# Neighbour search in segments, all aligned aggregation tiles on VectorE, longer lists in two blocks, one-hots on ScalarE

## The chip, the cores and the metric

The kernel runs on one core of one Trainium2 chip. The metric is the device time of one execution in microseconds (us); the median of several executions counts. One execution was also recorded by the hardware profiler. TensorE (PE in the profile) multiplies matrices, VectorE (DVE), ScalarE (ACT) and GpSimd (POOL) work elementwise, SyncE (SP) issues DMA transfers; GpSimd also issues the indirect DMA transfers (gathers).

## The reference

```python
# layer 0: graph convolution; adj is 2048 x 2048, sparse, random weights, diagonal present
A_norm = A + eye(n)
deg = A_norm.sum(0) + A_norm.sum(1) - diagonal(A_norm)
A_hat = A_norm * deg[:, None]**-0.5 * deg[None, :]**-0.5
agg = einsum('nm,bmd->bnd', A_hat, x)                  # x: 8 x 2048 x 256
h = relu(batchnorm(agg @ W1.T + b1)); o = batchnorm(h @ W2.T + b2)
x = layernorm(x + o)
# layer 1: attention over the neighbours only, 4 heads of 64
q, k, v = split(x @ W)
scores = q @ k.T / 8 + where(adj == 0, -inf, 0)
x = layernorm(x + softmax(scores) @ v)
```

All is fp32. Rows with small numbers have many neighbours, later rows few, since the edge probability falls with both indices.

## The kernel before

The 2048 nodes are cut into 16 blocks of 128 rows. Blocks 0 and 1 (`DENSE = 2`) are aggregated by a dense product; blocks 2 to 15 through lists of neighbours. In layer 1, block 0 attends densely and blocks 1 to 15 through the lists.

A list has two kinds of entries, called tiles; one tile is one gather of 128 rows. `ELL[t]` tiles of block t are *aligned*: tile i holds the i-th neighbour of each of the 128 rows. What rows have beyond `ELL[t]` neighbours is packed into `CAP[t]` *left-over* tiles, in which each partition belongs to some row of the block; for those a 128x128 one-hot matrix, made from the row numbers `qi1`, puts each entry back into its row. `LISTS` holds (ELL, CAP) for each block.

The order of instructions on each engine is the order in which the program writes them (`manual_schedule`); small generators are advanced by `next(...)` at chosen places. The stages, with their place in the profiled execution:

- **First stage, 0 to 72 us.** Sixteen 1 MB pieces of the adjacency matrix are loaded (L412) into 16 slots of 8 KB per partition. ScalarE and TensorE add up rows and columns (L416, L435). From the fourth piece on, one search step is taken for each piece (L442). Then a VectorE copy of the column sums (L447) starts the short sequence that gives `dinv` (L458, the inverse roots of the degrees), and the lists of blocks 2 and 3 are made (`list_steps`).
- **Dense product, 72 to 184 us.** For each of 16 pieces of x: load, scale by `dinv` (L472), store to `xs_d` (L473), 16 matrix instructions (L476). Two or three search steps go with each piece (L480).
- **Aggregation through lists and first linear layer, 184 to about 600 us** (pool `l0`). A loop over 116 tiles. Each tile gathers 128 rows of 8 KB from `xs_d` (L537) into a free slot. A tile that is *mine* is accumulated by VectorE in one pass over 128x2048 elements (L608 for the first of a block, L612 for the others); any other goes through TensorE with a weighted one-hot or diagonal matrix (L621, 8 instructions). `on_vector(t)` says how many aligned tiles of a block VectorE takes. At a block's end `add_rows` (L355) joins both parts, and `turn_steps` and `linear_steps` (transposes L394, products L377, statistics L371) are queued; `do_work(1 + mine)` advances them at each tile. One search step is taken at each tile (L588) as long as any is left. `gather_ahead` issues up to 10 gathers ahead, while enough slots are free; a block's slot is free once its search is done.
- **Second linear layer, about 600 to 830 us** (pool `l1`), with the seven-product scheme: `W[1]` to `W[4]` are sums and differences of quarters of W2, made on GpSimd (L667 to L670) from `w2s`, which is loaded at the stage's start (L656).
- **Attention, 830 to 2202 us.** Four passes of two batch entries each, and in a pass one step for each of 132 tiles. `score` (L1213 product, L1215 reduction, on VectorE) works 5 tiles ahead, `exps` (L1224, ScalarE) 4 ahead, `weigh_values` 3 ahead: the left-over tile's one-hot (L1230, VectorE) and the weighted values, on ScalarE for two of five tiles (three of five in the last pass; eight instructions, L1239) and else on VectorE (one instruction, L1244). `add_up` (L1255, TensorE) adds the tile to its rows. Keys and values are gathered 10 tiles ahead (L1195), queries of left-over tiles too (L1201). Projections of the next pass and the attention of block 0 are spread over the steps as side tasks.

**The search before.** `search_steps` handles one block after the other, 2 to 15 and then 1. It overwrites the block's rows by descending numbers where an edge is (L219), then takes `ROUNDS[t]` rounds over all 2048 columns: the eight largest (`max`, L223), and between rounds their removal (`match_replace`, L226). Each of these is one step: 2 x `ROUNDS[t]` steps for a block, 80 in all.

Of the kernel before, what the change touches and what calls it, by code (L numbers as in the profile page):

```python
# [27 lines left out]

LISTS = (
    None,  # L30
    (9, 7), (9, 5), (8, 3), (8, 2), (6, 3), (7, 2), (6, 2), (6, 2),
    (4, 3), (5, 2), (5, 2), (5, 2), (6, 1), (4, 2), (4, 2),
)
MAXNB = 32
ROUNDS = (0, 4, 3, 3, 3, 3, 3, 3, 3, 3, 2, 2, 2, 2, 2, 2)


@with_exitstack
def tile_gcn_then_masked_attention(
# [69 lines left out]
    idx = cpool.tile([P, NCOL], I32, name="idx")  # L109
    idxq = cpool.tile([P, NEDGE], I32, name="idxq")  # L110
    qi1 = cpool.tile([P, NEDGE], F32, name="qi1")
    padb = cpool.tile([P, NCOL], F32, name="padb")
    lbad = cpool.tile([P, 1], F32, name="lbad")
    iota_q1 = cpool.tile([P, P], F32, name="iota_q1")
# [64 lines left out]
    small = left.enter_context(tc.tile_pool(name="small", bufs=1, side="left", reuse_waits="tile"))  # L179
    st1 = small.tile([P, NH, NALL, 6], F32, name="st1")  # L180
    w1s = small.tile([P, ND, H], F32, name="w1s")
    over = small.tile([P, 3, NT], F32, name="over")
    lists = middle.enter_context(
        tc.tile_pool(name="lists", bufs=1, side="left", reuse_waits="tile")
    )
# [28 lines left out]
    def search_steps():  # L214

        for t in (*range(2, NT), 1):
            s = rows_of.pop(t)
            a = s.t
            nc.vector.scalar_tensor_tensor(a, a, 0.0, down, op0=ALU.not_equal, op1=ALU.mult)  # L219
            yield  # L220
            for r in range(ROUNDS[t]):
                m8 = nbx[:, t, 8 * r : 8 * r + 8]
                nc.vector.max(out=m8, in_=a)  # L223
                if r + 1 < ROUNDS[t]:
                    yield
                    nc.vector.match_replace(out=a, in_to_replace=m8, in_values=a, imm_value=0.0)  # L226
                else:
                    s.done()
                yield

    def list_steps(t, psum, name):

        r, m, cap, e0 = ELL[t], 8 * ROUNDS[t], CAP[t], edge0[t]
        here = slice(t, t + 1)
        ell = slice(col0[t], col0[t] + r)
        left_over = slice(col0[t] + r, col0[t] + r + cap)
        cols = slice(col0[t], col0[t] + r + cap)
        edges = slice(e0, e0 + cap)
# [26 lines left out]
        nc.vector.scalar_tensor_tensor(  # L265
            oh, iota_e[:, : cap * P], end[:, here], oh, op0=ALU.is_lt, op1=ALU.mult
        )
        yield
        yield
        pg = psum.tile([P, cap, MAXNB + 2 - r], F32, name=name)  # L270
        for i in range(cap):
            nc.tensor.matmul(
                pg[:, i, :], oh[:, i * P : (i + 1) * P], nbx[:, t, r:], start=True, stop=True
            )
        yield
        rank = lists.tile([P, cap], F32, name="rank")
        nc.vector.tensor_sub(rank, epos[:, :cap], pg[:, :, MAXNB - r])
        nc.vector.tensor_copy(qi1[:, edges], pg[:, :, MAXNB + 1 - r])
        for i in range(cap):
            c = left_over.start + i  # L280
            nc.vector.scalar_tensor_tensor(
                junk()[:, : m - r], iota_r[:, : m - r], rank[:, i : i + 1], pg[:, i, : m - r],
                op0=ALU.is_equal, op1=ALU.mult, accum_out=val[:, c : c + 1],
            )
        nc.vector.tensor_scalar(
            padb[:, cols], val[:, cols], 0.0, MASKED, op0=ALU.is_equal, op1=ALU.mult
        )
        key = lists.tile([P, MAXNB], F32, name="key")[:, : r + cap]
# [12 lines left out]
        nc.vector.scalar_tensor_tensor(  # L301
            fidx[:, left_over], q, float(N), key[:, r:], op0=ALU.mult, op1=ALU.add
        )
        nc.vector.tensor_scalar(wgt[:, ell], key[:, :r], rowid[:, here], None, op0=ALU.is_equal)
        nc.vector.tensor_tensor(wgt[:, left_over], key[:, r:], q, op=ALU.is_equal)
# [8 lines left out]
        )  # L314

    def on_vector(t):
        return 3 if t < 4 else ELL[t]

    def weights(t):

# [78 lines left out]
    with tc.tile_pool(name="first", bufs=1, side="right") as fp, tc.manual_schedule(  # L399
# [5 lines left out]
        with tc.tile_pool(name="pst", bufs=4, space=PSUM) as pst, tc.tile_pool(  # L405
# [3 lines left out]
            for t in range(NT):  # L409
# [29 lines left out]
                if not t:  # L439
                    rows_of.pop(0).done()  # L440
                if t > 2:
                    next(search)  # L442
            nc.sync.dma_start(w1s, w1t.rearrange("(c p) f -> p c f", p=P))
            for dst, src in params:
                nc.sync.dma_start(dst, src)
# [18 lines left out]
        with tc.tile_pool(name="ps_b", bufs=1, space=PSUM) as ps_b:  # L464
            pa = [banks(p) for p in (ps_a, ps_b)]
            for m in range(NT):
# [7 lines left out]
                for t in range(DENSE):  # L474
                    for c in range(QC):
# [1 line left out]
                            pa[t][c], at[:, t, m, :], xt[:, c * CH : (c + 1) * CH],  # L477
                            start=(m == 0), stop=(m == NT - 1),
                        )
                for _ in range(2 + m % 2):  # L480
                    next(search)
                if m < ELL[2] + CAP[2]:
                    gather_value(col0[2] + m)
                if m < ELL[3] + CAP[3]:
# [2 lines left out]
                weights(t)  # L487
            for t in range(DENSE):
                scale_rows(t, pa[t])

    with tc.tile_pool(name="l0", bufs=1, side="right", reuse_waits="tile") as lp, tc.tile_pool(
        name="psh", bufs=4, space=PSUM
# [78 lines left out]
        def turn_steps(t):  # L571
            for g in range(B // 2):
                turn_rows(t, g, psh)
                yield

        owed[0] = DENSE
        for _ in turn_steps(0):
            pass
# [6 lines left out]
        VLEAD, making = 16, []  # L585
        for n in range(len(tiles)):
            t, r, col, e, mine, k, count = tiles[n]
            next(search, None)  # L588
            for u in range(4, NT):
                if n == max(0, first[u] - VLEAD - 12):  # L590
                    making.append(list_steps(u, psh, "ph"))
# [42 lines left out]
            else:  # L634
                do_work(1 + mine)
        assert not making
        for f in work:
            for _ in f:
                pass
# [5 lines left out]
    with tc.tile_pool(name="l1", bufs=1, side="right", reuse_waits="tile") as lp, tc.tile_pool(  # L645
# [4 lines left out]
            for r in range(2):  # L650
                nc.sync.dma_start(hin[n][r].t, h_d[pairs[n][r]].rearrange("p f n -> p (f n)"))

        w2s = [lp.tile([P, 2, O], F32, name=f"w2s{j}") for j in range(2)]
        w2f = [lp.tile([P, 2, P], F32, name=f"w2f{j}") for j in range(4)]
        for j in range(2):
            nc.sync.dma_start(  # L656
                w2s[j], w2t[j * 2 * P : (j + 1) * 2 * P].rearrange("(c p) f -> p c f", p=P)
            )
        for n in range(TPC, TPC + 3):
            read_h(n)  # L660

        def w_half(i, j):
            return w2s[j][:, :, i * P : (i + 1) * P]

        W = {ij: w_half(*ij) for ij in HALVES}
        W[1], W[2], W[3], W[4] = w2f
        nc.gpsimd.tensor_add(W[1], W[1, 0], W[1, 1])  # L667
        nc.gpsimd.tensor_sub(W[2], W[1], W[0, 0])
        nc.gpsimd.tensor_sub(W[3], W[0, 0], W[1, 0])
        nc.gpsimd.tensor_sub(W[4], W[0, 1], W[2])  # L670

        st2 = lp.tile([P, NO, NALL, 6], F32, name="st2")
        bn1 = BatchNorm(lp, st1, g1s, be1s, sc1, sh1, "1")
# [118 lines left out]
            bn2.affine(o)  # L792
        nc.vector.tensor_reduce(lbad, over.rearrange("p a b -> p (a b)"), AX.X, ALU.add)

    left.close()


# [61 lines left out]
    def attention():  # L859

        with ExitStack() as st:
# [364 lines left out]
            def weigh_values(n):  # L1226
                e = tiles[n % NG][3]
                if e >= 0:
                    oh[n] = ep.tile([P, P], F32, name="oh", bufs=6)
                    nc.vector.tensor_scalar(  # L1230
                        oh[n], iota_q1, qi1[:, e : e + 1], None, op0=ALU.is_equal
                    )
                wv[n] = ep.tile([P, G2, NHEADS * VW], F32, name="wv", bufs=6)
                k, w = kg.pop(n), pw.pop(n)
                if n % 5 in (LAST_ON_ACT if n >= (NP - 1) * NG else ON_ACT):
# [467 lines left out]
```

## Time and profile before

| | |
|---|---|
| median of 14 runs | 2202.21 us (2199.77 to 2205.89) |
| the profiled execution | 2203.54 us, its span 2201.8 us |
| mean granted TensorE clock | 0.954 |
| busy share of the span | PE 90%, DVE 83%, POOL 66%, ACT 59% |
| DMA | 690.30 MB, mean 314 GB/s |
| search: L219, L223, L226 on VectorE | 34.1, 91.6 and 57.0 us busy |
| one-hots in attention, L1230 on VectorE | 160 instructions, 47.7 us busy |
| weighted values on ScalarE, L1239 | 1896 instructions, 477.3 us busy |

A matrix instruction of 128x512 elements shows about 0.6 us duration in the groups, but such instructions overlap: the chain of work that ended last shows eight of them (one tile, L621) in 3.43 us. In the same way a small VectorE or ScalarE instruction's duration is longer than the distance to the next one. So the distance between starts is read from the order of time where costs are added up.

### The profile page before, as it was taken

Reading aid. Unit: us, or ns where it says so; the run is one execution under the profiler, and the core shown is the slowest. Engines: PE = TensorE matmul, PEld = TensorE weight load, DVE = VectorE, ACT = ScalarE, POOL = GpSimd, SP = SyncE. Lnnn points to the kernel's source line nnn. Section 1 sums busy time; section 2 is a strip of 40 time slices with the busy share of each in tenths; the row PEclk is TensorE's granted clock in tenths of the full one; section 3 lists DMA queues with packets and bytes.
Section 4 is the critical chain, followed back from the end, with each engine's and each line's share of the span. In section 5 each row is a group of like instructions: output and inputs, shape, how many; then the busy total and the mean of one; then the engine's idle time right before and its main releaser. Section 6 shows DMA issues by size and latency. Waiting matters only on the chain.

```text
span 2201.8 us, 27916 instructions
## 1 busy us (share of the span) xinstructions
PE 1973.7 (90%) x7720; PEld 1277.9 (58%) x7720; DVE 1821.4 (83%) x3461; ACT 1302.0 (59%) x3896; POOL 1444.5 (66%) x1443
## 2 busy tenths in 40 slices
PE   5899989999999997979999999999999999687884
PEld 1444444445434444647776777777777777566663
DVE  6895999889856663229999999999999999989996
ACT  6331222223355534647777777877786877588875
POOL 2502668887457761137777787778786878878874
PEclk7899999999999998989999999999999999889996
DMA  8888899999648535569898999999999999999994
GB/s 323 287 306 308 342 344 354 356 382 405 249 174 288 168 87 205 193 244 338 329 371 331 355 354 365 363 339 379 325 365 349 358 355 340 349 372 359 332 346 152
DMA packets 261687, 690.30 MB, mean 314 GB/s; under 512 B 26385, under 2 KB 125457, under 8 KB 236433
## 3 DMA queue, kind: packets, MB, share of 16 engines
q0 software_dynamic: 109248, 442.68, 53.8%
q1 hardware_dynamic: 149968, 228.96, 29.3%
q10 hardware_dynamic: 2304, 16.78, 1.8%
q8 instruction: 64, 1.05, 0.2%
q14 instruction: 103, 0.84, 0.1%
HBM read 561.71 MB, written 126.62 MB: 313 GB/s over the span
## 4 chain that ended last, share of the span: by engine, by line
PE 48%; DVE 25%; ACT 8%; DMA 8%; issue 7%; POOL 3%; SPq 0%; DVEq 0%; ACTq 0%; POOLq 0%
PE pa L702 8%; PE ph L377 8%; PE pm L980 8%; DVE pr L1213 7%; PE pa L621 6%; PE po L1255 5%; PE pa L476 5%; ACT wv L1239 4%; DVE wv L1244 4%; DVE s L1215 4%; DMA kg<-kv_d,idx 2%; DMA e<-in_adj_dram 2%; DMA qg<-q_d,idxq 2%; ACT x L852 2%; POOL kg L1195 2%
## 5 line engine op out<-in xcount | busy, mean ns | idle before, releaser
L1195 POOL DMA_INDIRECT kg<-kv_d,idx x528 | 568.3, 1076 | 150.6 <-issue 81.3
L1239 ACT ACTIVATE wv<-kg,pw 128x65 f32<-128x65 f32 x1896 | 477.3, 336 | 0.0
L1255 PE MATMUL po<-wv,ident 128*128 128x260 f32 x1472 | 420.2, 399 | 49.1 <-DVE z L1069 47.6
L1215 DVE TENSOR_REDUCE s<-pr 128x8 f32<-128x512 f32 x528 | 362.1, 686 | 34.4
L980 PE MATMUL pm<-wq,x1t 128*128 128x512 f32 (+1 forms) x1024 | 374.4, 496 | 12.6 <-ACT x1t L925 12.4
L1255 PEld LDWEIGHTS po<-wv,ident 128*128 128x128 f32 x1472 | 276.9, 198 | 119.6 <-issue 69.8
L1224 ACT ACTIVATE pw<-s,padb 128x8 f32<-128x8 f32 x528 | 157.3, 299 | 223.2 <-DVE s L1215 221.9
L1213 DVE TENSOR_TENSOR pr<-qb,kg 128x512 f32<-128x512 f32 x368 | 260.1, 707 | 4.6 <-DMA kg<-kv_d,idx 2.5
L537 POOL DMA_INDIRECT e<-xs_d,idx x116 | 154.8, 1335 | 158.5 <-issue 82.9
L980 PEld LDWEIGHTS pm<-wq,x1t 128*128 128x128 f32 x1024 | 186.3, 192 | 104.2 <-issue 73.1
L377 PE MATMUL ph<-e,w1s 128*128 128x512 f32 x512 | 228.0, 593 | 0.8 <-ACT e L382 0.8
L1244 DVE TENSOR_TENSOR wv<-kg,pw 128x520 f32<-128x520 f32 x291 | 211.9, 728 | 2.4 <-ACT pw L1224 2.4
L1255 PE MATMUL po<-wv,oh 128*128 128x260 f32 x640 | 196.3, 397 | 8.7 <-DVE wv L1244 8.2
L1201 POOL DMA_INDIRECT qg<-q_d,idxq x160 | 164.5, 1028 | 48.8 <-issue 46.3
L311 POOL DMA_INDIRECT av<-in_adj_dram,fidx x116 | 154.4, 1331 | 44.1 <-issue 32.3
L382 ACT ACTIVATE h<-ph,b1s 128x512 f32<-128x512 f32 x96 | 66.0, 687 | 195.7 <-PE ph L377 194.6
L621 PE MATMUL pa<-e,wt 128*128 128x512 f32 x352 | 164.8, 612 | 0.0
L377 PEld LDWEIGHTS ph<-e,w1s 128*128 128x128 f32 x512 | 95.9, 190 | 115.4 <-issue 112.4
L1048 PEld LDWEIGHTS po<-kvr,p 128*128 128x128 f32 x1024 | 138.0, 198 | 30.9 <-ACT p L1037 21.8
L1029 PE MATMUL pm<-q,kt 128*128 128x256 f32 x512 | 137.6, 393 | 13.7 <-POOL q L932 9.4
L1048 PE MATMUL po<-kvr,p 128*128 128x65 f32 x1024 | 134.8, 276 | 15.4 <-ACT p L1037 15.2
L1255 PEld LDWEIGHTS po<-wv,oh 128*128 128x128 f32 x640 | 119.8, 198 | 38.0 <-issue 12.7
(190 smaller groups left out, 3362.5 us busy)
## 6 DMA issues: line engine op xcount, KB each, us to landing
kv_d<-kvr SPq DMA_DIRECT2D x32, 1032.0 KB, 6.9
h_d<-h SPq DMA_DIRECT2D x24, 1024.0 KB, 8.8
e<-h_d SPq DMA_DIRECT2D x24, 1024.0 KB, 7.2
e<-in_adj_dram SPq DMA_DIRECT2D x16, 1024.0 KB, 18.2
xt<-in_x_dram SPq DMA_DIRECT2D x16, 1024.0 KB, 7.9
xs_d<-xt ACTq DMA_DIRECT2D x16, 1024.0 KB, 7.4
y_d<-y SPq DMA_DIRECT2D x128, 128.0 KB, 2.2
yt<-y_d SPq DMA_DIRECT2D x32, 512.0 KB, 12.4
```

Of the source, the lines that this page charges most:

```text
L377: nc.tensor.matmul(ph, w1s[:, d, f * P : (f + 1) * P], as_agb(agb[t])[:, d, r * B // 2 : (r + 1) * B // 2, :], start=(d == 0), stop=(d == ...
L621: nc.tensor.matmul(pa[c], w, xg[n].t[:, c * CH : (c + 1) * CH], start=(k == 0), stop=(k == count - 1),)
L702: nc.tensor.matmul(py, w[:, f, :], t[:, f, :], start=(f == 0), stop=(f == 1))
L980: nc.tensor.matmul(pm, x1t[b, c][:, d, i * P : (i + 1) * P], rhs(d), start=(d == 0), stop=(d == ND - 1),)
L1048: nc.tensor.matmul(po0[b][:, h, :], p[:, h, :], heads(kvr[b, c][:, i, D:])[:, h, :], start=(j == 0 and h == 0), stop=(j == NT - 1), skip_g ...
L1195: nc.gpsimd.indirect_dma_start(out=kg[n].rearrange("p b e -> p (b e)"), out_offset=None, in_=kv_d[p][:], in_offset=bass.IndirectOffsetOnAx ...
L1201: nc.gpsimd.indirect_dma_start(out=qg[n].rearrange("p b e -> p (b e)"), out_offset=None, in_=q_d[p][:], in_offset=bass.IndirectOffsetOnAxi ...
L1213: nc.vector.tensor_mul(pr, q, kg[n][:, :, :D])
L1215: nc.vector.tensor_reduce(s.rearrange("p b h -> p (b h)"), pr.rearrange("p b (h e) -> p (b h) e", e=HD), AX.X, ALU.add,)
L1239: nc.scalar.activation(wv[n][:, b, hs], k[:, b, D:][:, hs], AF.Copy, scale=w[:, b, h : h + 1],)
L1244: nc.vector.tensor_mul(wv[n].rearrange("p b (h e) -> p b h e", e=VW), k[:, :, D:].rearrange("p b (h e) -> p b h e", e=VW), w[:, :, :, None ...
L1255: nc.tensor.matmul(po[p, t, b].rearrange("p h e -> p (h e)"), oh[n] if e >= 0 else ident, wv[n][:, b, :], start=(r == 0), stop=(r == ELL[t ...
```

## The change

- `search_steps` cuts the 2048 columns into 16 segments (12 for blocks from 10 on) and takes the eight largest of each by short `max` instructions into `best` (128x128 or 128x96); a reduction keeps the largest of the eighth values in `over[:, 3]`, so that a full segment is noticed at the end; the rounds then run over `best`. A block is four steps, 60 in all.
- Two search steps for each piece from the fourth on in the first stage (one before), three for each piece of the dense product (two or three before), none in the aggregation loop.
- `on_vector(t)` is `ELL[t]` for all blocks; it was 3 for blocks 2 and 3.
- `LISTS`: block 1 from (9, 7) to (12, 4), block 2 from (9, 5) to (10, 3). A pass has 131 tiles in place of 132, and 35 left-over tiles in place of 40.
- The one-hots of attention: two ScalarE instructions each, Square of (iota - qi1) and Relu of (1 - that), with the new `qn1 = -qi1`.
- `w2s` is loaded at the start of pool `l0`, and `W[1]` to `W[4]` are made at its end.

```diff
-    (9, 7), (9, 5), (8, 3), (8, 2), (6, 3), (7, 2), (6, 2), (6, 2),
+    (12, 4), (10, 3), (8, 3), (8, 2), (6, 3), (7, 2), (6, 2), (6, 2),
...
+SEGMENTS = (
+    (0, 8, 32, 72, 128, 200, 288, 392, 512, 648, 800, 968, 1152, 1352, 1568, 1800, 2048),
+    (0, 14, 57, 128, 228, 356, 512, 697, 910, 1152, 1422, 1721, 2048),
+)
...
+            parts = SEGMENTS[t >= 10]
+            n = len(parts) - 1
+            best = lists.tile([P, 16, 8], F32, name="best", bufs=2)[:, :n]
+            for i, (u, v) in enumerate(zip(parts, parts[1:])):
+                nc.vector.max(out=best[:, i, :], in_=a[:, u:v])
+                if i == n // 2:
+                    yield
+            s.done()
+            yield
+            nc.vector.tensor_reduce(over[:, 3, t : t + 1], best[:, :, 7], AX.X, ALU.max)
+            best = best.rearrange("p a b -> p (a b)")
             for r in range(ROUNDS[t]):
                 m8 = nbx[:, t, 8 * r : 8 * r + 8]
-                nc.vector.max(out=m8, in_=a)
+                nc.vector.max(out=m8, in_=best)
                 if r + 1 < ROUNDS[t]:
-                    yield
-                    nc.vector.match_replace(out=a, in_to_replace=m8, in_values=a, imm_value=0.0)
-                else:
-                    s.done()
-                yield
+                    nc.vector.match_replace(
+                        out=best, in_to_replace=m8, in_values=best, imm_value=0.0
+                    )
+            yield
...
+        nc.vector.tensor_scalar(qn1[:, edges], qi1[:, edges], -1.0, None, op0=ALU.mult)
...
     def on_vector(t):
-        return 3 if t < 4 else ELL[t]
+        return ELL[t]
...
                 if t > 2:
-                    next(search)
+                    for _ in range(2):
+                        next(search)
...
-                for _ in range(2 + m % 2):
-                    next(search)
+                for _ in range(3):
+                    next(search, None)
...
-            next(search, None)
...
-                    nc.vector.tensor_scalar(
-                        oh[n], iota_q1, qi1[:, e : e + 1], None, op0=ALU.is_equal
+                    nc.scalar.activation(
+                        oh[n], iota_q1, AF.Square, bias=qn1[:, e : e + 1]
                     )
+                    nc.scalar.activation(oh[n], oh[n], AF.Relu, bias=ones[:, :1], scale=-1.0)
```

More of the change, by code (lines that the diff above doesn't have):

```diff
@@ L111, in tile_gcn_then_masked_attention @@
     qi1 = cpool.tile([P, NEDGE], F32, name="qi1")
+    qn1 = cpool.tile([P, NEDGE], F32, name="qn1")
     padb = cpool.tile([P, NCOL], F32, name="padb")
@@ L181, in tile_gcn_then_masked_attention @@
     w1s = small.tile([P, ND, H], F32, name="w1s")
-    over = small.tile([P, 3, NT], F32, name="over")
+    over = small.tile([P, 4, NT], F32, name="over")
     lists = middle.enter_context(
@@ L489, in tile_gcn_then_masked_attention, with w_half @@
                 scale_rows(t, pa[t])
+    keep = ExitStack()
+    wp = keep.enter_context(tc.tile_pool(name="w2", bufs=1, side="right", reuse_waits="tile"))
+    w2s = [wp.tile([P, 2, O], F32, name=f"w2s{j}") for j in range(2)]
+    w2f = [wp.tile([P, 2, P], F32, name=f"w2f{j}") for j in range(4)]
+    def w_half(i, j):
+        return w2s[j][:, :, i * P : (i + 1) * P]
+    W = {ij: w_half(*ij) for ij in HALVES}
+    W[1], W[2], W[3], W[4] = w2f
     with tc.tile_pool(name="l0", bufs=1, side="right", reuse_waits="tile") as lp, tc.tile_pool(
@@ L574, in turn_steps @@
                 yield
+        for j in range(2):
+            nc.sync.dma_start(
+                w2s[j], w2t[j * 2 * P : (j + 1) * 2 * P].rearrange("(c p) f -> p c f", p=P)
+            )
         owed[0] = DENSE
@@ L636, in tile_gcn_then_masked_attention @@
         assert not making
+        nc.gpsimd.tensor_add(W[1], W[1, 0], W[1, 1])
+        nc.gpsimd.tensor_sub(W[2], W[1], W[0, 0])
+        nc.gpsimd.tensor_sub(W[3], W[0, 0], W[1, 0])
+        nc.gpsimd.tensor_sub(W[4], W[0, 1], W[2])
         for f in work:
@@ L651, in read_h @@
                 nc.sync.dma_start(hin[n][r].t, h_d[pairs[n][r]].rearrange("p f n -> p (f n)"))
[L653 to L658, printed above, removed]
         for n in range(TPC, TPC + 3):
             read_h(n)
[L662 to L670, printed above, removed]
         st2 = lp.tile([P, NO, NALL, 6], F32, name="st2")
@@ L793, in tile_gcn_then_masked_attention @@
         nc.vector.tensor_reduce(lbad, over.rearrange("p a b -> p (a b)"), AX.X, ALU.add)
+    keep.close()
     left.close()
```

## The prediction

> **What bounds the kernel now.** I read the chain of waits over the whole span, then the windows, then the order of time at the seams that the edits touch. A difference within 0.2% (4.4 us) can't be told from no change here.
>
> First stage, order of time on VectorE and what follows. Columns: start, duration, engine, line, and in brackets the idle time ahead with its releaser.
>
> ```profile
> 51.95 2.29 DVE L223 MAX8 nbx<-e 128x8 f32<-128x2048 f32 x1
> 54.16 2.27 DVE L219 SCALAR_TENSOR_TENSOR e<-e,down 128x2048 f32<-128x2048 f32 x1
> 57.21 0.69 DVE L447 COPY junk<-pc 128x512 f32<-128x512 f32 x1 [0.78 <-ACT junk L416]
> ...
> 62.39 2.00 ACT L472 ACTIVATE xt<-xt,dinv 128x2048 f32<-128x2048 f32 x1 [4.92 <-POOL dinv L141]
> ```
>
> The search ends at 56.43, just as the last adjacency piece has been summed; L447 is next in VectorE's order, and `dinv`, the lists and the dense product hang on it. There is no more than 0.8 us of slack: more search ahead of L447 moves everything behind.
>
> The dense product (72 to 184) is 256 matrix instructions in 111.7 us with PE busy all the time; work beside it is free. Then the aggregation, groups in the window 184 to 296, in which blocks 2 and 3 are aggregated (their last `add_rows` end at 248.4 and 298.3). Columns: line, engine, operation, count | busy us, mean ns | idle.
>
> ```profile
> L223 DVE MAX8 nbx<-e 128x8 f32<-128x2048 f32 x13 | 29.6, 2279 | 0.0
> L226 DVE MATCH_REPLACE8 e<-nbx,e 128x2048 f32<-128x2048 f32 x7 | 16.0, 2290 | 0.0
> L219 DVE SCALAR_TENSOR_TENSOR e<-e,down 128x2048 f32<-128x2048 f32 x5 | 11.4, 2277 | 0.0
> L612 DVE SCALAR_TENSOR_TENSOR e<-e,wgt,e 128x2048 f32<-128x2048 f32 x4 | 9.4, 2344 | 0.0
> L621 PE MATMUL pa<-e,wt 128*128 128x512 f32 x151 | 68.3, 595 | 0.0
> L377 PE MATMUL ph<-e,w1s 128*128 128x512 f32 x92 | 42.0, 593 | 0.0
> ```
>
> PE does mostly list tiles there, VectorE mostly search; from 184 to 260 the chain of waits is 98% PE (L621 59%, L377 32%, L394 7%). From block 5 on there is no search left and DMA runs at 0.95 to 1.0 with 380 to 420 GB/s: 28 us for 9 tiles. That part the change leaves alone.
>
> Attention: windows for passes 1 to 3 and the last pass (length, busy us of PE, PEld, DVE, ACT, POOL, granted clock, DMA share, GB/s), and the end of one tile's work in order of time.
>
> ```profile
> 1000.00:1870.00 870.00, 824.91 (x3964) 638.36 (x3963) 824.56 (x1699) 663.04 (x2289) 666.71 (x756) 0.99 0.95 352
> 1870.00:2180.00 310.00, 239.25 (x1078) 188.95 (x1076) 281.07 (x557) 242.60 (x925) 247.82 (x246) 0.89 0.94 337
> ```
> ```profile
> 1319.49 0.28 DVE L1230 TENSOR_SCALAR oh<-iota_q,qi 128x128 f32<-128x128 f32 x1
> ...
> 1319.69 0.69 DVE L1244 TENSOR_TENSOR wv<-kg,pw 128x520 f32<-128x520 f32 x1
> ```
>
> VectorE is busy 95% in the first three passes and has hardly any long wait (13 us of named waits in 870), so it sets the pace, with PE (95%) and DMA (0.95) close behind. ScalarE has a quarter free. A one-hot holds VectorE 0.20 us, from its start to the next one's.
>
> **Part by part.** *First stage, search.* What a short MAX8 costs no row shows. L265 takes 0.88 us at 640 columns and 0.48 at 256: 1.04 ns a column, so 2.13 us for 2048. A MAX8 of 2048 lasts 2.29, but the next independent instruction starts after 2.20 (184.83 to 187.03). So the fixed part of each segment is 0.07 (by distance) to 0.16 us (by duration); below that I allow zero. I take 0.07, since segments don't depend on each other. A step that needs the one before costs 0.19 extra (L256 to L257 to L258, one column each). A block of three rounds: 2.32 (L219) + 2.13 + 16 x 0.07 + 0.2 (reduction) + three maxima and two replacements of 128 columns at 0.32 and two value loads at 0.08 = 7.5 us, against 6 x 2.3 = 13.9 now; with two rounds 6.4 against 9.3. The 26 steps of the first stage are now blocks 2 to 7 whole and half of block 8: 6 x 7.5 + 3.6 = 48.6 us. They begin at 26.23 as now (after the copies L424) and end at 74.9, 18 us after today's 56.4; the adjacency has long landed, nothing hides it. Block 2's shorter left-over list (3 tiles, not 5) takes 1.6 us off the sequence from L447 to L476 (L262 0.54 to 0.41, L265 0.88 to 0.62, L272 ten instructions in 2.30 to six, two L281 at 0.15). **+16 us**; +5 if segments have next to no fixed cost, +26 with 0.16.
> The Trainium skill speaks against this edit: its page "VectorE: DVE Perf Modes", in the section on the TRN2 errata, says that small tiles pay a fixed latency each, 151 cycles by its measured formula, 157 ns. By that the 105 segments would cost 9 us more and the sum would end at 2177.
>
> *Dense product.* 34 steps are left, under 60 us of VectorE beside 112 us of PE; before, 40 steps were 92. Nothing on the path. If that cover were gone, it would be 60 us; it has 50 to spare.
>
> *Aggregation.* 27 full-width steps (62 us of VectorE) leave this loop, 12 aligned tiles go to VectorE (12 x 2.34 = 28 us), and 13 tiles (one is dropped) leave TensorE at 3.43 us each by the chain of waits: 45 us. Block 2, 64 us now: PE 3 x 3.43 + 16 products at 1.72 + transposes 2 + lists 1.6 = 41; VectorE 1.3 + 9 x 2.3 + 2.7 (L355) + 16 statistics at 0.61 + two lists at 3.7 + 1.4 = 43; DMA 13 tiles and 4 MB of `h` at 390 GB/s = 46, with a start of up to ten gathers instead of seven, as all search slots are free. These interlock: 48 us, saving 16 (10 to 20). Block 3, 50 us now: PE 28, VectorE 32, DMA 35: saving 15 (9 to 18). Block 4, 35 now: two search steps go, DMA wants 32: saving 3 (0 to 5). **-32 us** (-19 to -43 with the early gathers). What is late next is DMA.
>
> *Attention.* Per pass 5 left-over tiles and one tile less. VectorE: 160 one-hots x 0.20 = 32 us, 4 tiles at 1.8 (L1213, L1215, L1244) = 7: 39 in all, 29 of it in three passes where VectorE decides, 10 in the last. DMA: 20 x 262 KB + 4 x 528 KB = 7.3 MB, 20 us at 355 GB/s. ScalarE gains 140 pairs. The nearest rows for 128x128: 0.40 (L556), 0.29 (L417), and 0.25 between starts of 128x65 (eight in 2.01, L1239). The Relu needs the Square, so 0.5 to 0.8 a pair; I take 0.7: 98 us, 74 of it in 870, so ScalarE 76% to 88%; the last pass 78% to 86%, 92% in its middle (84% now). A pair stands in ScalarE's queue ahead of the next `exps` (L1224), on which VectorE's L1244 waits two steps later. Bounds: -36 if VectorE's time comes back whole, +12 if ScalarE's queue costs a third of a pair's time more than VectorE gives. I take **-18**: half of the 29, as PE and DMA stand at 0.95 too, and 3 in the last pass.
>
> *At no cost:* `qn1`, 15 instructions of 0.17 us under the list work; the `w2s` loads, on SP's queue now ahead of the first `h` store at 201 (their space is free at 184); W1 to W4 on POOL, 2.9 us, after the last gather as before (POOL idles 26 us ahead of L667), first used at 624.7.
>
> Sum against the profiled execution, 2203.5 (span 2201.8 and 1.7 around it): +16 - 32 - 18 = 2169.5; the median lies 1.3 below that execution: **2168**.
>
> **Rivals.** *More comes back:* VectorE's 36 in attention, segments cheap (+8), 40 in the aggregation: 2134 to 2145. For it: 13 us of waits in 870. Against: DMA at 0.95.
> *It cancels:* segments at 0.16 (+26), DMA holds blocks 2 and 3 (-19), attention -6: about 2203. For it: no short MAX8 is in the trace.
> *Slower: ScalarE's queue decides in attention.* From the point where the pair delays `exps` so that VectorE waits; ScalarE's reserve is its wait for L1215, 222 us in all. If half of the pairs' 98 us comes onto the path and half of the gain goes: +49 - 9 + 16 - 32 = +24, 2226. From a net loss of 16 in attention on, the kernel is slower. For it: in-order ScalarE at 92% in the last pass, with 2.0 us bursts (L1239). Against: 3 to 5 tiles of lead.
> *Table switches:* one row shows the price.
>
> ```profile
> L416 ACT ACT_TABLE_LOAD x1 | 1.3, 1283 | 0.8 <-PEq L1686 0.8
> ```
>
> One load serves Copy, Identity, Relu and Exp; Square is not in this trace. If it needed another table, 280 loads are 359 us of ScalarE, beyond its reserve: 2400 and more.
> The Trainium skill ("ScalarE: Activation LUTs", "Table sets: the hidden batching unit") names relu, copy, identity and abs as in every set, not square; by its 2.66 us a switch it would be 745 us.
>
> **How the numbers follow.** Forecast 0.56 (own range 2146 to 2192), more 0.17, cancels 0.10 (0.03 faster, 0.06 same, 0.01 slower), ScalarE 0.14, tables 0.03. Faster 0.76, same 0.06, slower 0.18. The range 2140 to 2208 leaves out the low half of "more" and most of the slower cases.
>
> **What would show it.** L447 near 75 instead of 57, the dense product 16 us later and as long; MAX8 of segments a mean distance near 0.2 us; the last `add_rows` of blocks 2 and 3 48 and 83 us after the dense product ends (64 and 114 now); no wait of VectorE for `exps`; one table load. Wrong if L447 stays, if block 2 keeps 60 us, or if VectorE waits for L1224.

## The result and the profile after

The changed kernel takes **2171.09 us** (median of 6 runs, 2166.06 to 2174.16); the kernel before, in 28 runs beside and ahead of it, takes 2203.22 us. The ratio is 0.9855, with an interval of 0.9843 to 0.9866. The profiled execution took 2175.57 us, with a span of 2173.8 us (before: 2203.54 and 2201.8). That one is 4.5 us above the median of its kernel, so the two traces differ by 28.0 us and the medians by 32.1. The prediction said 2168.

I read the seams first, in the order of time, and place each stage's end there. A block ends with its last `add_rows`. "First score" is the end of the first L1213 (L1233 after) of attention.

| us from the span's start | before | after | difference of the stage |
|---|---|---|---|
| copy of the column sums starts (L447, after: L464) | 57.2 | 75.1 | +17.9 |
| dense product on PE, starts of its first and last instruction | 71.9 to 183.0 | 88.4 to 201.0 | +1.5 (111.1, 112.6) |
| its last result scaled | 184.4 | 202.4 | +18.0 in all so far |
| blocks 2, 3, 4, each from the end of the one before | 64.6, 49.4, 34.6 | 47.4, 36.2, 31.7 | -17.2, -13.2, -2.9 |
| blocks 5 to 8 | 28.2, 28.8, 27.6, 29.9 | 31.0, 29.1, 31.8, 30.1 | +7.5 |
| block 15 ends | 599.5 | 591.0 | -26.5 for the aggregation |
| first score | 979.7 | 965.6 | -5.6 in between |
| end | 2201.8 | 2173.8 | -13.9 for attention |

The first stage, order of time on VectorE (start, duration, engine, line, then shapes and count): one block of search, and the seam at which the search hands over to the copy.

```profile
27.54 2.29 DVE L224 SCALAR_TENSOR_TENSOR e<-e,down 128x2048 f32<-128x2048 f32 x1 [2.25 <-PE pc L451]
29.86 3.19 DVE L230 MAX8 best<-e 128x8 f32<-128x8 f32 x16
33.09 0.18 DVE L235 TENSOR_REDUCE over<-best 128x1 f32<-128x16 f32 x1
33.19 0.28 DVE L239 MAX8 nbx<-best 128x8 f32<-128x128 f32 x1
...
34.82 2.27 DVE L224 SCALAR_TENSOR_TENSOR e<-e,down 128x2048 f32<-128x2048 f32 x1
...
71.52 2.27 DVE L224 SCALAR_TENSOR_TENSOR e<-e,down 128x2048 f32<-128x2048 f32 x1
73.83 1.31 DVE L230 MAX8 best<-e 128x8 f32<-128x8 f32 x9
75.06 0.68 DVE L464 COPY junk<-pc 128x512 f32<-128x512 f32 x1
```

Sixteen short MAX8 over 2048 columns in all take 3.19 us, 0.20 each; a block takes 7.28 us (27.54 to 34.82). The last line is the copy for which everything waits: VectorE reaches it without a gap, straight out of the ninth segment of block 8. The search does set this time.

The aggregation of blocks 2 and 3, groups in the window 202 to 286 (line, engine, operation, count | busy us, mean ns | idle and releasers).

```profile
L393 PE MATMUL ph<-e,w1s 128*128 128x512 f32 x96 | 42.7, 595 | 0.0
L643 DVE SCALAR_TENSOR_TENSOR e<-e,wgt,e 128x2048 f32<-128x2048 f32 x16 | 37.4, 2337 | 0.0
...
L652 PE MATMUL pa<-e,wt 128*128 128x512 f32 x48 | 22.8, 619 | 0.0
```

The search (57 us in the like window before) is gone, VectorE's accumulations rose from 4 to 16, and PE's list tiles fell from 151 instructions to 48. Now the windows: blocks 2 and 3, blocks 4 to 7, attention in passes 1 to 3 and in the last pass. The columns are length, busy us of PE, PEld, DVE, ACT and POOL, granted clock, DMA share, GB/s.

```profile
202.00:286.00 84.00, 73.19 (x221) 37.41 (x222) 71.11 (x141) 23.52 (x37) 49.51 (x38) 0.94 1.01 416
286.00:420.00 134.00, 116.31 (x326) 59.79 (x325) 116.57 (x240) 34.23 (x53) 110.91 (x76) 0.90 0.95 360
1000.00:1870.00 870.00, 818.48 (x3919) 630.71 (x3918) 803.28 (x1577) 719.32 (x2471) 665.60 (x745) 0.99 0.95 349
1870.00:2150.00 280.00, 223.21 (x1026) 177.88 (x1024) 254.49 (x472) 249.11 (x943) 220.78 (x224) 0.90 0.94 344
```

In blocks 2 and 3 no engine is above 87% busy, but DMA is full (1.01, 416 GB/s). It does not hold these blocks alone: of the chain of waits in this window PE still has 57% (L393, L652, L410; before it had 98% from 184 to 260), and the gathers av and e (L327, L565) have 18%. In attention VectorE went from 824.6 to 803.3 us in an equal window, ScalarE from 663.0 to 719.3 (83%).

### The profile page after: what moved, and what is told of

Its sections match the earlier page's. It is cut to its first block, busy times and chain, and to the rows that moved or that the text cites. A ratio compares the mean times of both kernels' runs of the same rounds, so it can differ in the third digit from the quotient of the medians.

```text
span 2173.8 us, 27900 instructions
## 1 busy us (share of the span) xinstructions
PE 1932.7 (89%) x7590; PEld 1259.1 (58%) x7590; DVE 1737.2 (80%) x3537; ACT 1379.6 (63%) x4145; POOL 1435.0 (66%) x1417
## 4 chain that ended last, share of the span: by engine, by line
PE 43%; DVE 19%; ACT 14%; DMA 13%; issue 6%; POOL 4%; SPq 0%; DVEq 0%; ACTq 0%; POOLq 0%
PE pa L721 8%; PE pm L1000 7%; PE ph L393 7%; ACT wv L1260 7%; PE pa L493 5%; PE po L1276 5%; DVE pr L1233 4%; DMA x<-in_x_dram 4%; PE pa L652 4%; DVE s L1235 3%; DVE wv L1265 3%; ACT x L872 2%; DMA kg<-kv_d,idx 2%; POOL kg L1215 2%; DMA qg<-q_d,idxq 2%
## 5 line engine op out<-in xcount | busy, mean ns | idle before, releaser
L1215 POOL DMA_INDIRECT kg<-kv_d,idx x524 | 560.1, 1069 | 144.1 <-issue 81.3
L1276 PE MATMUL po<-wv,ident 128*128 128x260 f32 x1536 | 436.8, 397 | 41.2 <-DVE z L1089 39.0
L1276 PEld LDWEIGHTS po<-wv,ident 128*128 128x128 f32 x1536 | 288.2, 197 | 106.0 <-issue 56.1
L1233 DVE TENSOR_TENSOR pr<-qb,kg 128x512 f32<-128x512 f32 x384 | 273.6, 713 | 8.7 <-DMA kg<-kv_d,idx 6.4
L565 POOL DMA_INDIRECT e<-xs_d,idx x115 | 166.6, 1449 | 120.2 <-DMA xs_d<-xt 62.9
L1244 ACT ACTIVATE pw<-s,padb 128x8 f32<-128x8 f32 x524 | 155.4, 298 | 133.4 <-DVE s L1235 132.9
L393 PE MATMUL ph<-e,w1s 128*128 128x512 f32 x512 | 226.8, 594 | 0.8 <-ACT e L398 0.8
L1265 DVE TENSOR_TENSOR wv<-kg,pw 128x520 f32<-128x520 f32 x289 | 209.7, 725 | 2.1 <-PE po L1276 1.1
L327 POOL DMA_INDIRECT av<-in_adj_dram,fidx x115 | 152.0, 1322 | 46.6 <-issue 29.0
L1276 PE MATMUL po<-wv,oh 128*128 128x260 f32 x560 | 173.4, 394 | 2.4 <-DVE wv L1265 1.3
L1221 POOL DMA_INDIRECT qg<-q_d,idxq x140 | 142.9, 1021 | 42.7 <-issue 39.6
L643 DVE SCALAR_TENSOR_TENSOR e<-e,wgt,e 128x2048 f32<-128x2048 f32 x70 | 163.8, 2340 | 0.2
L393 PEld LDWEIGHTS ph<-e,w1s 128*128 128x128 f32 x512 | 95.6, 190 | 113.7 <-issue 110.7
L1096 POOL TENSOR_TENSOR x<-z,x 128x256 f32<-128x256 f32 x126 | 125.1, 993 | 46.4 <-DVE z L1089 44.6
```

The costliest lines, as they stand in the source:

```text
L393: nc.tensor.matmul(ph, w1s[:, d, f * P : (f + 1) * P], as_agb(agb[t])[:, d, r * B // 2 : (r + 1) * B // 2, :], start=(d == 0), stop=(d == ...
L565: nc.gpsimd.indirect_dma_start(out=xg[n].t, out_offset=None, in_=xs_d[:], in_offset=bass.IndirectOffsetOnAxis(ap=idx[:, col : col + 1], ax ...
L643: nc.vector.scalar_tensor_tensor(agr[t].t, xg[n].t, wgt[:, col : col + 1], agr[t].t, op0=ALU.mult, op1=ALU.add,)
L1215: nc.gpsimd.indirect_dma_start(out=kg[n].rearrange("p b e -> p (b e)"), out_offset=None, in_=kv_d[p][:], in_offset=bass.IndirectOffsetOnAx ...
L1233: nc.vector.tensor_mul(pr, q, kg[n][:, :, :D])
L1265: nc.vector.tensor_mul(wv[n].rearrange("p b (h e) -> p b h e", e=VW), k[:, :, D:].rearrange("p b (h e) -> p b h e", e=VW), w[:, :, :, None ...
```

## The experiments

The experiments ran on three occasions, each on another chip, and on the first two the times were about 1% longer (the changed kernel took 1225.2 us from the first score to the end there, 1208.2 in the trace above; the stages that PE or VectorE bound were as long): the kernel before measured 2225.67 us with e1 to e4, 2226.35 with r_after, e6, e9 and e10, and 2203.70 with e11 to e14. So each is compared by its ratio to the kernel before there, or with the changed kernel there: **r_after**, a repeat, took 2189.80 us, a ratio of 0.9838 (0.9821 to 0.9854). It ran with e6, e9 and e10; for e1 to e4 it stands in, as the kernel before took 0.7 us less there. On the third occasion the result above (0.9855, 2171.09) serves.

> The changed kernel unchanged, as the reference of the runs beside it. The stages that TensorE and VectorE bound should repeat within 1 us (L464 at 75, blocks 2 and 3 in 47 and 36 us); attention passes may differ by some us from chip to chip if DMA has a part in them, and not if VectorE alone sets their pace.

**e1: one search step for each piece.** The rest of the search goes into the dense product.

```diff
-                    for _ in range(2):
-                        next(search)
+                    next(search)
```

> The changed kernel with one search step per adjacency piece in the first stage instead of two (13 steps there, 47 beside the dense product). Theory (the search ahead of L464 sits on the path, and VectorE has room beside the dense product): the copy L464 starts near 57 us instead of 75.1, the dense product ends 17 to 18 us earlier, all that follows moves by as much, about 2154 us. Rival (the first stage is held by something else, or the search that moves runs out past the dense product and delays block 4's list): L464 moves but the aggregation's start or first block grows by the same amount, 2166 to 2172 us.

2174.98 us, ratio 0.9758 (0.9739 to 0.9776): 15 us below r_after (18 by the ratios). Order of time on VectorE:

```profile
58.64 0.69 DVE L463 COPY junk<-pc 128x512 f32<-128x512 f32 x1 [6.69 <-ACT junk L432]
```

The copy starts at 58.6 again, and now VectorE had been idle 6.69 us until ScalarE's sums were there. The dense product begins at 72.0 (88.4 after the change), and blocks 2 to 8 take 237.7 us in all (237.3). So the second search step in the first stage is a pure loss of some 15 us; the dense product hides all of it.

**e3: three aligned tiles on VectorE in blocks 2 and 3, as before.**

```diff
-        return ELL[t]
+        return 3 if t < 4 else ELL[t]
```

> The changed kernel with VectorE taking three aligned tiles of blocks 2 and 3 as before, so that TensorE has 12 more tiles at 3.43 us (41 us). Theory (blocks 2 and 3 were bound by TensorE): block 2 takes 47 + 7 x 3.4 = about 60 to 64 us (47.4 in the changed kernel), block 3 36 + 10 = 46 to 50 us (36.2), 25 to 35 us slower, about 2200. Rival (the search on VectorE was what held these blocks, and TensorE had room): the blocks grow by less than 10 us together, about 2178.

2210.06 us, ratio 0.9929 (0.9911 to 0.9946): 20 us above r_after. Blocks 2 and 3 take 59.4 and 48.8 us. The window over both:

```profile
201.00:310.00 109.00, 108.90 (x305) 52.20 (x306) 44.47 (x126) 25.16 (x46) 45.77 (x45) 1.00 0.88 346
```

PE is busy 108.90 of 109 us, VectorE 44. With the search gone but the tiles still on TensorE, block 2 gains 5 us and block 3 only 0.6; the move gives the other 12 and 13. Even of the 5 us, one tile less on TensorE (the new list of block 2; 3.43 us a tile) would explain most.

**e13: the converse, on the kernel before.** All aligned tiles on VectorE, the old search still in the loop.

```diff
-        return 3 if t < 4 else ELL[t]
+        return ELL[t]
```

> The kernel before with one edit alone: all aligned tiles of blocks 2 and 3 on VectorE, 11 more there, while the search of the last six blocks stays in the same loop. Theory (VectorE's room in these blocks comes from the search having left): blocks 2 and 3 become bound by VectorE, 41 + 32 us of their own and 62 of search, 125 to 140 us instead of 114, and the whole 10 to 25 us slower than before. Rival (TensorE's relief of 11 tiles, 38 us, decides): blocks 2 and 3 take 85 to 100 us, the whole 10 to 30 us faster.

2212.90 us, ratio 1.0040 (1.0027 to 1.0053), 9 us slower. Blocks 2 and 3 take 71.5 and 54.1 us:

```profile
186.00:311.00 125.00, 85.44 (x235) 41.96 (x236) 123.06 (x169) 23.28 (x37) 69.67 (x50) 0.83 0.83 311
```

Here VectorE is the one that is full, 123.06 of 125 us, and PE waits. Neither edit is worth much by itself (5.8 us, and a loss); together they save 30 us in these two blocks.

**e11: adjacency values gathered earlier.** In blocks 5 to 7 the changed kernel gives 7 us back. Two waits stood out there, waits in the window 286 to 440 (engine, tile and line, releaser: us, times, longest):

```profile
DVE wgt L339 <- DMA av<-in_adj_dram,fidx: 10.2, 2, 6.1
```

```diff
-            v = n + VLEAD
-            if first[4] <= v < len(tiles):
-                gather_value(tiles[v][2])
+            while n > 7 and valued[0] < min(n + 21, len(tiles)):
+                gather_value(tiles[valued[0]][2])
+                valued[0] += 1
```

> The changed kernel with the adjacency values of list tiles (av, L327) gathered 20 tiles ahead of their block's turn instead of 16. Theory (after the change the DMA queue is full from 202 to 286 us, the small av gathers land behind rows of xs_d, and the weights L339 wait for them, 10.2 us in two waits in blocks 5 and 7): these waits go, blocks 5 to 7 take 28 to 29 us each instead of 29 to 35, 4 to 8 us off the whole. Rival (DMA has only fallen behind, and the rows of xs_d would be late instead): the wait moves to the row tiles, blocks 4 to 8 keep their sum within 2 us.

2171.30 us, ratio 0.9856 (0.9835 to 0.9878): no change. The named wait shrank, and others came in its place (waits of e11, 281 to 436):

```profile
DVE wgt L339 <- DMA av<-in_adj_dram,fidx: 2.9, 1, 2.9
DVE e L643 <- DMA e<-xs_d,idx: 1.7, 1, 1.7
PE pa L652 <- DMA e<-xs_d,idx: 3.4, 2, 2.7
```

Blocks 3 to 8 take 188.0 us against 189.9. So that one wait does not hold them. A hint at what does lies in the windows of blocks 5 to 8, before and after (columns as above):

```profile
333.00:447.40 114.40, 102.76 (x296) 50.58 (x295) 103.14 (x218) 31.07 (x48) 95.20 (x64) 0.95 0.95 355
```
```profile
317.70:439.70 122.00, 105.08 (x296) 53.46 (x295) 103.76 (x223) 31.09 (x48) 100.43 (x71) 0.91 0.95 362
```

PE's and VectorE's work is as before, but DMA moves 44.2 MB in place of 40.6 (length times GB/s), at the same share. Where blocks 2 and 3 are slow, as in e3 (108 us) and e13 (126 us), blocks 5 to 8 take 115.5 and 114.6 us; in the eleven other traces after the change, where blocks 2 and 3 take 81 to 87 us, they take 119 to 124. This fits transfers that the fast blocks 2 and 3 leave behind: 3.6 MB more at 355 GB/s are 10 us, and 7 come back.

**e2: the one-hots back on VectorE.**

```diff
-                    nc.scalar.activation(
-                        oh[n], iota_q1, AF.Square, bias=qn1[:, e : e + 1]
+                    nc.vector.tensor_scalar(
+                        oh[n], iota_q1, qi1[:, e : e + 1], None, op0=ALU.is_equal
                     )
-                    nc.scalar.activation(oh[n], oh[n], AF.Relu, bias=ones[:, :1], scale=-1.0)
```

> The changed kernel with the one-hots of attention back on VectorE (one instruction each, 140 in all). Theory (VectorE's time decides in attention, a one-hot costs it 0.20 us and about half of that comes back): 10 to 18 us slower than the changed kernel, about 2185, with the last pass changed little. Rival 1 (all of it counts): 28 us slower, 2199. Rival 2 (DMA or ScalarE's queue holds attention, so that the pairs on ScalarE cost what VectorE gained): within 5 us of the changed kernel, or faster, above all in the last pass, where ScalarE is busy 89%.

2201.95 us, ratio 0.9890 (0.9872 to 0.9907): 12 us above r_after, where 140 one-hots at 0.20 us are 28 us of VectorE. Just under half of VectorE's time counts.

**e6: no one-hots at all** (every left-over tile is added with the identity).

```diff
-                    oh[n] = ep.tile([P, P], F32, name="oh", bufs=6)
-                    nc.scalar.activation(
-                        oh[n], iota_q1, AF.Square, bias=qn1[:, e : e + 1]
-                    )
-                    nc.scalar.activation(oh[n], oh[n], AF.Relu, bias=ones[:, :1], scale=-1.0)
+                    oh[n] = ident
```

> The changed kernel with the one-hots of attention left out on both engines; left-over tiles use the identity, so their entries go to wrong rows. It shows what the pairs cost on ScalarE. Theory (ScalarE's queue has room in passes 0 to 2 and little in the last): passes 0 to 2 within 4 us of the changed kernel together, the last pass 3 to 8 us shorter. Rival (ScalarE's queue holds attention: 98 us more work there): 15 to 40 us shorter, spread over all passes.

2190.75 us, ratio 0.9842 (0.9828 to 0.9856): the same as r_after, and attention takes 1224.1 us against 1225.2. The 280 ScalarE instructions cost nothing that can be measured; the 3 to 8 us expected for the last pass do not show.

**e4: the old lists of blocks 1 and 2.**

```diff
-    (12, 4), (10, 3), (8, 3), (8, 2), (6, 3), (7, 2), (6, 2), (6, 2),
+    (9, 7), (9, 5), (8, 3), (8, 2), (6, 3), (7, 2), (6, 2), (6, 2),
```

> The changed kernel with the list lengths of before, (9, 7) and (9, 5) for blocks 1 and 2: five left-over tiles and one tile more in each attention pass, and block 2 of the aggregation with 9 tiles on VectorE and 5 on TensorE. Theory: +1.6 us ahead of the dense product, +2 to +5 us in block 2, and in attention 4 tiles and 20 gathers of queries more, 7.3 MB, 20 us of DMA at 355 GB/s, of which half to all counts: 14 to 26 us slower, 2185 to 2197. Rival (attention is held by VectorE or ScalarE's queue and not by DMA: 4 tiles at 1.8 us and 20 one-hot pairs on ScalarE): 7 us there, 11 to 14 us slower in all, about 2183.

2223.71 us, ratio 0.9991 (0.9978 to 1.0003): 34 us above r_after. Its profiled execution, at 2217.2 one of the lowest of 12, is 24 above r_after's profiled one (which is 3.7 above its own median): 5.5 in block 2, 15.7 in attention, 3 elsewhere. Ten of the 34 no trace shows. The lists, the smallest-looking edit, are worth more than the one-hots.

**e9: x for the projections loaded 12 steps ahead, not 8.** VectorE's longest waits in attention after the change (window 1000 to 1870):

```profile
DVE x L916 <- DMA x<-in_x_dram: 13.8, 4, 5.0
DVE lo_nm L866 <- POOL lo_rs L146: 9.3, 8, 1.7
DVE pr L1233 <- DMA qg<-q_d,idxq: 5.2, 12, 1.0
```

```diff
-                projection(at, p, starts, int(steady), 8)
+                projection(at, p, starts, int(steady), 12)
```

> The changed kernel with the loads of a projection's inputs (yt and x) in attention passes 1 to 3 issued 12 tiles ahead of their use instead of 8. Theory (after the change the projection waits for x, whose load takes 21 to 26 us on the chain of waits, where 8 + 2 steps are some 23 us): VectorE's wait for x (13.8 us in passes 0 to 2) falls below 3 us and passes 0 to 2 get 8 to 15 us shorter together. Rival (DMA's bandwidth as such sets the pace there and a load that starts earlier delays the gathers by as much): the wait for x goes, waits for kg and qg or the idle time of VectorE grow, the passes stay within 4 us.

2188.62 us, ratio 0.9823 (0.9807 to 0.9839), not to be told from r_after. But r_after's trace, on the same occasion, has no such wait in its attention window, so the run doesn't test my theory that these loads hold the pace; it stays open.

**e10 and e12: what does a left-over tile's query gather cost?** e10 leaves the 140 query gathers out and scores with the block's own rows; e12 keeps their number and halves their bytes (rows of 1 KB from x in place of 2 KB queries).

```diff
-                if e >= 0:
-                    qg[n] = ep.tile([P, G2, D], F32, name="qg", bufs=5)
...
-                q = qb[p, t] if e < 0 else qg.pop(n)
+                q = qb[p, t]
```

> The changed kernel without the gathers of queries for left-over tiles (those tiles use the block's own query rows, so their scores are wrong): 140 x 262 KB = 36.7 MB less DMA, and 140 issues of 1.02 us less on GpSimd, with the work of VectorE, ScalarE and TensorE as it is. Theory 1 (DMA holds attention next to VectorE): 20 to 60 us shorter, most of it in passes 0 to 2. Theory 2 (VectorE alone sets the pace there, 92 to 95% busy): below 15 us, from the waits for x and qg alone.

```diff
-                        out=qg[n].rearrange("p b e -> p (b e)"), out_offset=None, in_=q_d[p][:],
+                        out=qg[n], out_offset=None, in_=x[0],
...
-                q = qb[p, t] if e < 0 else qg.pop(n)
+                q = qb[p, t] if e < 0 else qg.pop(n)[:, None, :].to_broadcast([P, G2, D])
```

> The changed kernel with the gathers of queries for left-over tiles kept in number but half as large: 1 KB rows of the input x instead of 2 KB rows of the queries, used for both batch entries (their scores are wrong). 18.4 MB less DMA, the same 140 issues on GpSimd. It divides the 56 us that the run without these gathers was shorter. Theory (bytes of DMA decide): 20 to 30 us shorter than the changed kernel. Rival (GpSimd's 140 issues of 1.02 us, in its queue ahead of the gathers of keys and values): less than 6 us shorter.

e10: 2133.32 us, ratio 0.9582 (0.9569 to 0.9596), 56 us below r_after, 0.40 us a gather. e12: 2169.13 us, ratio 0.9847 (0.9825 to 0.9869), 2 us below the changed kernel and not to be told from it. In the traces its attention is 5 to 9 us shorter than in e11 and after, for 18.4 MB that take 53 us at 349 GB/s. So half of the bytes cost next to nothing, and the gathers as a whole cost much. The two runs stand on different occasions, and neither was repeated on the other's. The same window in e10 and then in e12:

```profile
1000.00:1870.00 870.00, 827.00 (x3976) 640.94 (x3974) 805.02 (x1615) 731.05 (x2516) 581.80 (x660) 0.99 0.89 328
```
```profile
1000.00:1870.00 870.00, 819.85 (x3939) 635.22 (x3937) 810.02 (x1590) 722.79 (x2483) 669.43 (x750) 0.99 0.93 337
```

The column that differs most is POOL: 582 us against 669. Its in-order queue issues every gather. After the change, GpSimd's waits in this window (the first and third are the time to issue a gather, on top of its 665.6 us busy):

```profile
POOL kg L1215 <- issue: 56.4, 229, 0.7
POOL ln_rs L144 <- DVE ln_mv L858: 38.8, 15, 8.4
POOL qg L1221 <- issue: 27.7, 91, 0.3
POOL x L1096 <- DVE z L1089: 27.1, 16, 5.5
```

and in e10:

```profile
POOL ln_rs L144 <- DVE ln_mv L858: 69.0, 18, 9.2
POOL x L1096 <- DVE z L1089: 65.9, 33, 8.7
POOL kg L1215 <- issue: 62.4, 230, 0.9
```

In the changed kernel GpSimd works or issues 750 of 870 us, and in what is left it waits for VectorE, with more gathers queued behind that wait. In e10 those waits double: it has slack. VectorE's instructions are shorter too with fewer gathers (groups, after and then e10):

```profile
L1233 DVE TENSOR_TENSOR pr<-qb,kg 128x512 f32<-128x512 f32 x271 | 193.7, 715 | 4.4 <-DMA kg<-kv_d,idx 2.9
```
```profile
L1227 DVE TENSOR_TENSOR pr<-qb,kg 128x512 f32<-128x512 f32 x380 | 261.1, 687 | 2.8 <-DMA kg<-kv_d,idx 0.6
```

28 ns on 524 products, and 27 on 289 weighted values (L1265, 725 and 698 ns), are 22 us of VectorE's time, at most that much of the 56. For the rest, the DMA queue that carries the gathers says something (packets, MB, share of 16 engines; r_after, e12, e10):

```profile
q0 software_dynamic: 106896, 434.28, 53.2%
```
```profile
q0 software_dynamic: 102416, 415.93, 52.1%
```
```profile
q0 software_dynamic: 95696, 397.57, 50.2%
```

A query gather is 80 packets, one of half the bytes 48. e12 drops 40% of these packets and saves next to nothing, so their number is an unlikely cause too. GpSimd's in-order queue is the suspect that is left; no run tests it alone.

**e14: what the runs point to.** The changed kernel with e1 and e11, and longer lists everywhere: 23 left-over tiles in a pass in place of 35, 130 tiles in place of 131, TensorE taking a few of the aligned ones.

```diff
-    (12, 4), (10, 3), (8, 3), (8, 2), (6, 3), (7, 2), (6, 2), (6, 2),
-    (4, 3), (5, 2), (5, 2), (5, 2), (6, 1), (4, 2), (4, 2),
+    (14, 2), (11, 2), (9, 2), (8, 2), (7, 2), (6, 2), (7, 1), (7, 1),
+    (4, 3), (6, 1), (6, 1), (6, 1), (6, 1), (5, 1), (5, 1),
...
-        return ELL[t]
+        return (0, 12, 10, 8, 8, 6, 6, 6, 6, 4, 5, 5, 5, 6, 4, 4)[t]
```

> The changed kernel with one search step per piece in the first stage, av gathered 20 tiles ahead, and longer lists throughout: 23 left-over tiles and 107 aligned ones in a pass instead of 35 and 96, none filled above 0.85, with as many tiles on VectorE in the aggregation as before. 14.7 MB less DMA in attention. Theory (DMA's bytes and VectorE each count about half in attention): 15 to 17 us from the first stage, 4 to 8 from av, 15 to 25 from the lists, some 40 us less than the changed kernel beside it, a ratio of 0.963 to 0.970 to the kernel before. Rival (attention does not follow the bytes once they fall that little): 20 to 25 us less, 0.973.

**2128.99 us** (2126.57 to 2133.11), ratio 0.9662 (0.9642 to 0.9681), faster than both kernels: 42 us less than the changed one. The copy starts at 58.5, and attention takes 1182.4 us (1208.2). By e10, 48 query gathers fewer are 19 us, and 4 tiles fewer at 2.3 (1208.2 for 524 tiles, a mere average) are 9: 28, against the 26 measured. It is the only run of the third occasion that speaks for the 0.40 us, together with other changes.

## Why the prediction was right, and where its steps were off

**First stage (+16): right.** L464 was put at 74.9 and is at 75.06; the dense product starts 16.5 us later, and its cover over the rest of the search held. It is 1.5 us longer in this trace, which makes the 18.0 of the table; in r_after, the same kernel, it is 111.0 us, so that is no effect of the change. Two small misses cancel: the search begins at 27.54, not 26.23, and a block takes 7.28 us, not 7.5. The fixed part of a segment is what I took from the distance between starts: 3.19 us less 2.13 for the columns, over 16, is 0.07. The Trainium skill, which I weighed against it ("VectorE: DVE Perf Modes", TRN2 errata), says that many small tiles pay their latency tile by tile. Here its 157 ns show only in how long one instruction lasts: the short MAX8 last 0.29 us in the mean, but independent ones follow each other at 0.20. The distance decided, and this term with the page's 157 ns would have been 9 us too high. My lower bound of +5 was wrong by my own terms: 105 segments at 0.07 are 7 us, so without a fixed cost it is +9. e1 shows that the whole term could have been avoided.

**Aggregation (-32): right in blocks 2 to 4, not behind them.** Forecast 48 us for block 2 and savings of 16, 15 and 3; measured 47.4, and 17.2, 13.2, 2.9. e3 and e13 confirm the mechanism: first PE was the bound, and the tiles could leave it only because the search left VectorE. "What is late next is DMA" held at once (416 GB/s at 1.01), with PE still on most of the chain. But I had written of the later blocks "that part the change leaves alone". They gave 7 us back: not through one wait (e11), and by the windows of blocks 5 to 8 through transfers left behind by the faster blocks 2 and 3. My 380 to 420 GB/s "from block 5 on" was too high as well, blocks 5 to 8 have 355 before. The three savings add up to 34, not to the 32 that I put into the sum. So the stage brings 26.5.

**Attention (-18): right in size, with a wrong reason.** By the traces it is 13.9, or 19.5 with the 5.6 us between the aggregation's end and the first score; these 5.6 I hadn't listed, and they vary (371.8 to 378.5 us in other runs, 380.2 before). They are not the earlier loading of `w2s`, as the last matrix instruction of the second linear layer starts 222.3 us after block 15 before and 222.5 after: that edit brought nothing, as forecast. The one-hots came out as I weighed them: nearly half of 28 us (12). The term that was mis-sized is the lists: I took half of 7 us of VectorE, and held 20 us of DMA for the 7.3 MB behind it. e12 shows that such bytes cost next to nothing. What counts is 20 query gathers at 0.40 us and 4 tiles at 2.3, 17 us; e4's trace has 15.7. GpSimd, 77% busy in my own row, does not occur in my weighing of VectorE against PE and DMA, though its queue issues each of these gathers. With the one-hots' 12 that makes 28 us, which is also what the medians leave where both were measured (36.5 less 8.5 for the stages ahead). On the third occasion the medians leave 23.6 and the traces at most 19.5. Why the occasions differ by that much stays open. That -18 lies so near to the traces is luck in part: the lists stood in it with 3 us and measured 16.

**The sum:** forecast +16 - 32 - 18 = -34; by the two traces +18.0 - 26.5 - 5.6 - 13.9 = -28.0; by the medians of 2171.09 and 2203.22 -32.1. Term by term the traces are +2.0, +5.5 and -1.5 off (the last with the 5.6 in it). The medians come closer to the forecast than the traces do because the trace after was taken on a longer execution than its median.

**The rivals.** *ScalarE's queue* is refuted by e6, and VectorE's waits for `exps` (L1244) come to 0.2 us after the change in the window 1000 to 1870. ScalarE's reserve can be read, its wait for scores, before and after, in that window.

```profile
ACT pw L1224 <- DVE s L1215: 158.0, 139, 3.3
```
```profile
ACT pw L1244 <- DVE s L1235: 100.8, 85, 3.9
```

The pairs came out of this wait; 101 us of it are left. In the order of time a pair costs what I took, 0.74 (1302.07 to 1302.81):

```profile
1302.07 0.40 ACT L1250 ACTIVATE oh<-iota_q,qn 128x128 f32<-128x128 f32 x1
1302.50 0.40 ACT L1253 ACTIVATE oh<-oh,ones 128x128 f32<-128x128 f32 x1
1302.81 0.35 ACT L1037 COPY kt<-pm 128x256 f32<-128x256 f32 x1
```

*Table switches:* there is one load, as before, so Square needs none.

```profile
L432 ACT ACT_TABLE_LOAD x1 | 1.3, 1283 | 0.8 <-PEq L1707 0.8
```

*It cancels* needed segments at 0.16 and DMA holding blocks 2 and 3 at a saving of 19; neither came. *More comes back* needed VectorE to be the only bound of attention; e2 gives 12 of 28.

## What to carry to other kernels

Before work is moved off a full engine, see what frees its new place: each half of this pair did next to nothing without the other. Put moved work under a stage whose bound is another engine, not under the last instruction that everything waits for, even if the stage looks half idle. And test what a gather costs by its number and by its bytes apart; here two lists with fewer gathers were worth more (24 to 34 us) than the one-hots (12 us).

## What was not expected of the hardware

- Without its 140 query gathers the kernel was 0.40 us shorter for each (e10), but with rows of 1 KB in place of 2 KB only 2 us in all (e12, on another occasion), although the DMA share stands at 0.95. That share of busy time is not a limit by bytes: in the aggregation the same engines moved 416 GB/s at 1.01, in attention 349 at 0.95.
- VectorE's 128x512 product lasts 715 ns with the query gathers in the kernel and 687 without them (e10). Why was not tested.
- TensorE's granted clock in blocks 2 and 3 was lower where it had more idle time: 1.00 at 99.9% busy (e3), 0.94 at 87% (after), 0.83 at 68% (e13). A short stretch need not follow this: 0.97 at 82% from 260 to 280 us (after).
